# Moving whole expert sets into the last two thirds of the following row's slot

## The chip, the cores and the metric

The kernel runs on one core of a Trainium2 chip. The core has four engines that compute: TensorE (PE in the profile, with its weight loads as PEld), VectorE (DVE), ScalarE (ACT) and GpSimd (POOL). SyncE (SP) issues nearly all of this kernel's transfers. Each engine works through its own queue in order and waits on semaphores that the others raise. The metric is the time of one launch in microseconds (us) on the device. Three runs of the kernel before gave 1374.11, 1378.02 and 1379.18 us, a median of 1378.02 us.

## The reference

The input is 4 rows of 512 tokens with 128 channels, all fp32. Two layers are applied. Cut to what matters here:

```python
xn = layernorm(x)                                   # layer 0
x  = x + band_attention(xn) + gated_experts(xn)     # 16 heads, window of 64; 16 experts, top 4
xn = layernorm(x)                                   # layer 1
x  = x + full_attention(xn) + relu_experts(xn)      # 16 heads, 512 keys; 8 experts, top 2

def relu_experts(xf):
    score = relu(xf @ rw1 + rb1) @ rw2 + rb2
    gate  = softmax(top 2 of score)                 # 0 for the other six experts
    out   = sum over e of gate[:, e] * (relu(xf @ W1[e] + b1[e]) @ W2[e] + b2[e])
```

In the band attention of layer 0 the logit of a query and each of its 64 predecessors is not a dot product: it goes through two GELU networks on the difference of two 16-vectors per head. So each row needs 64 large subtractions on VectorE and as many GELUs on ScalarE. The relu experts of layer 1 are 4 hidden blocks and 4 second products for each of 8 experts and each row, all computed for every token, with the gate deciding what counts.

## The kernel before

Everything is laid out by row of the batch. A row's relu experts and its full attention belong to layer 1, but both need only this row's finished layer 0 result, so the kernel starts the experts of one row while the next row's layer 0 is under way.

The work is written as Python generators, each of which yields after a small step. `weave` (L92, `woven` at L80) takes pairs of a generator and a number of steps and interleaves them in proportion, so that all end together. A generator that has made its number of steps is left where it is and can be continued in a later weave. The tile framework gives each instruction a priority by its place in this program order; a planner then puts the ready instructions of each engine into its queue by priority, using its own estimates of durations. Instructions can so move ahead of their place when an engine would be free. The small products of the band logits (L574) are lifted in priority by `tc.high_priority` (L570). Once the queues are written they are run strictly in order.

The generators:

- `band_logits(b)` (L543): 64 steps, each one subtraction on VectorE (L560), its GELU on ScalarE (L562 or L566) and four small products on TensorE (L574). Then a maximum, an exponential (L616, L620) and the write of the weights to DRAM, `by_t` (L621).
- `band_values(b)` (L304): needs `by_t`. For each of four token tiles: eight loads `f` from `by_t` (L312), transposes (L321), copies `g` (L322), a write to `by_s` (L327), loads `wb` in skewed order (L338), products with the values (L348, L352). 14 steps; it ends in `add_rows`.
- `gated_experts(b)` (L647): layer 0's 16 experts, one step each (L674, L681, L659 to L663), with loads of `wT` (L630) and of the routes (L672).
- `prepare(b)` (L492): norms, projections and routes of layer 0, 6 steps.
- `relu_experts(b)` (L392): layernorm and transposes, the router (L381 with `rw1`, L406), the routes (L416), then the experts: each step makes one hidden block (`hidden`, L378: a 128x512 product at L381 and a relu at L389) for expert e and one second product (L442) for expert e-1. Expert e loads `w1` (L428), `w2` (L430) and its route `r` (L432). After each expert VectorE weighs the result (L446) and GpSimd adds it up (L447). In layer 0 the generator makes 3 steps before the experts and 36 for them. In layer 1, where the list `pace` is in use, each of the 36 is two steps, and the hidden products are tied to the attention's steps.
- `full_attention()` (L769): layer 1's attention for all rows, with an order of products written out by hand. A step makes score products of one pair for the maxima (`m`) and of another for the exponentials (`x`) (L920), VectorE takes maxima (L936), ScalarE exponentials (L942), and every other step multiplies by the values (L838).

The PSUM banks that `bank()` (L107) hands out are two, shared by the relu experts, the band values, the preparation and the transposes. `full_attention` has its own six.

A row's slot in layer 0 is two weaves, `first` and `second` (L719 to L734). From row 1 on, `first` holds 30 steps of the row's own band logits, 7 gated experts and all band values of the row before. `second` holds the other 37 steps of logits, 10 of gated experts, the preparation of the next row and 20 steps of the relu experts of the row before. The remaining 21 steps of those experts lie in `first` of one slot later, or, for row 2, in layer 1: there they are woven with the band values of row 3, and the experts of row 3 follow (L950 to L953). "First part" and "second part" below mean these two weaves.

Of the kernel before, what the change touches and what calls it, by code (L numbers as in the profile page):

```python
# [29 lines left out]
B, T, C = 4, 512, 128  # L30
# [49 lines left out]
def woven(*tracks):  # L80


    live = [[g, n, 0] for g, n in tracks]
    while live:
        t = min(live, key=lambda v: (v[2] + 1) / v[1])
        t[2] += 1
        if next(t[0], "end") == "end" or t[2] == t[1]:
            live.remove(t)
        yield


def weave(*tracks):  # L92
    for _ in woven(*tracks):
        pass
# [3 lines left out]
def two_layers(ctx: ExitStack, tc: tile.TileContext, w: dict, consts: bass.AP, out: bass.AP):  # L98
# [8 lines left out]
    def bank():  # L107
        return ps_f.tile([P, 512], FP, tag="f", name="bank")
# [16 lines left out]
    def c_(name):  # L125
        return cst[:, offs[name][0]:offs[name][1]]
# [80 lines left out]
    def layernorm(b, dst, pin=False):  # L207

        mv = small.tile([P, TPB, 2], FP, tag="mv", name="mv")
        for i in range(TPB):  # L210
            st = small.tile([P, 6], FP, tag="st", name="st")
            ins = nc.vector.bn_stats(st, x1[:, b * TPB + i, :])
            if pin and not i:
                tc.keep_in_program_order(ins)
            nc.vector.bn_aggr(mv[:, i, :], st)
        rs = inv_sqrt(mv[:, :, 1], 1.0)
        for i in range(TPB):
            nc.vector.tensor_scalar(
                dst[:, i, :], x1[:, b * TPB + i, :], mv[:, i, 0:1], rs[:, i:i + 1],
                ALU.subtract, ALU.mult,  # L220
            )
# [9 lines left out]
    def transposed(src):  # L231

        pt = bank()
        for i in range(TPB):
            nc.tensor.transpose(pt[:, i * P:(i + 1) * P], src[:, i, :], ident)
        return pt

    def routes(pool, tag, g, n, k, less, dst):


        shape = [P, TPB, n, n]
        both = pool.tile([P, 2, TPB, n * n], FP, tag=tag, name="both")
        gt, eq = both[:, 0], both[:, 1]
        other = g[:, :, None, :].to_broadcast(shape)
        own = g[:, :, :, None].to_broadcast(shape)
        gt4 = gt.rearrange("p t (a b) -> p t a b", a=n)
        eq4 = eq.rearrange("p t (a b) -> p t a b", a=n)
        nc.vector.tensor_tensor(gt4, other, own, ALU.is_gt)
        nc.vector.tensor_tensor(eq4, other, own, ALU.is_equal)
        nc.vector.tensor_tensor(eq, eq, less[:, None, :].to_broadcast([P, TPB, n * n]), ALU.mult)  # L250
        nc.vector.tensor_tensor(gt, gt, eq, ALU.add)
        rank = small.tile([P, TPB, n], FP, tag=f"rank{n}", name="rank")
        nc.vector.tensor_reduce(rank, gt4, AX.X, ALU.add)
        nc.vector.tensor_scalar(rank, rank, float(k), None, ALU.is_lt)
        mx = small.tile([P, TPB], FP, tag="rmx", name="rmx")
        nc.vector.tensor_reduce(mx, g, AX.X, ALU.max)
        nc.vector.tensor_tensor(dst, g, mx[:, :, None].to_broadcast([P, TPB, n]), ALU.subtract)
        nc.scalar.activation(dst, dst, AF.Exp)
        nc.vector.tensor_tensor(dst, dst, rank, ALU.mult)
        nc.vector.tensor_reduce(mx, dst, AX.X, ALU.add)  # L260
        nc.vector.reciprocal(mx, mx)
        nc.vector.tensor_tensor(dst, dst, mx[:, :, None].to_broadcast([P, TPB, n]), ALU.mult)
# [18 lines left out]
    def add_rows(b, py):  # L281
        nc.vector.tensor_tensor(rows_of(b), rows_of(b), py, ALU.add)
# [95 lines left out]
    def hidden(wt, bias, b, c):  # L378

        ph = bank()  # L380
        mm = nc.tensor.matmul(ph, wt[:, c * P:(c + 1) * P], xT[:, b * T:(b + 1) * T], start=True, stop=True)  # L381
        if pace:
            tc.add_manual_dep(
                mm.ins, pace[-1].ins.name,
                mybir.DependencyInfo(mybir.DependencyClass.NoSync, mybir.DependencyReason.DATA),
                reason="experts spread over the steps",
            )
        h = chain.tile([P, T], FP, tag="h", name="h", bufs=5)
        nc.scalar.activation(h, ph, AF.Relu, bias=bias[:, c:c + 1])  # L389
        return h  # L390

    def relu_experts(b):  # L392


        xn = chain.tile([P, TPB, C], FP, tag="o", name="xn", bufs=1)
        layernorm(b, xn)
        pt = transposed(xn)
        nc.scalar.copy(xT[:, b * T:(b + 1) * T], pt)
        yield
        rw1 = chain.tile([C, F1], FP, tag="ew1", name="rw1")  # L400
        nc.sync.dma_start(out=rw1, in_=w["L1_ffn_rw1"])
        hs = [hidden(rw1, cols[:, 32:36], b, c) for c in range(4)]
        pg = bank()
        for i in range(TPB):
            for c in range(4):
                nc.tensor.matmul(  # L406
                    pg[:, i * E1:(i + 1) * E1], hs[c][:, i * P:(i + 1) * P], rw2[:, c, :],
                    start=(c == 0), stop=(c == 3),
                )
        scores = small.tile([P, TPB, E1], FP, tag="scores1", name="scores1")  # L410
        nc.vector.tensor_tensor(
            scores, pg[:, :TPB * E1].rearrange("p (t e) -> p t e", e=E1),
            rb2[:, None, :].to_broadcast([P, TPB, E1]), ALU.add,
        )
        route = small.tile([P, TPB, E1], FP, tag="route1", name="route1")
        routes(small, "pairs", scores, E1, K1, c_("lt8"), route)  # L416
        yield
        rT = route_rows(small, route, E1, route_d[1][b], 1.0)
        py = bank()
        nc.tensor.matmul(py, b2_1, rT, start=True, stop=True)  # L420
        total = chain.tile([C, T], FP, tag="total", name="total", bufs=1)
        nc.scalar.copy(total, py)
        yield
        old = None
        for e in range(E1 + 1):
            if e < E1:
                w1 = chain.tile([C, F1], FP, tag="ew1", name="ew1")
                nc.sync.dma_start(out=w1, in_=w["L1_ffn_W1"][e])  # L428
                w2 = chain.tile([P, 4, C], FP, tag="ew2", name="ew2")
                nc.sync.dma_start(out=w2, in_=w["L1_ffn_W2"][e].rearrange("(c p) d -> p c d", p=P))  # L430
                r = chain.tile([P, T], FP, tag="r", name="r")
                nc.sync.dma_start(out=r, in_=route_d[1][b][e].partition_broadcast(P))  # L432
            new = []
            if old:
                py = bank()
            for c in range(4):
                if e < E1:
                    new.append(hidden(w1, cols[:, e * 4:e * 4 + 4], b, c))
                if pace:
                    yield  # L440
                if old:
                    nc.tensor.matmul(py, old[1][:, c, :], old[0][c], start=(c == 0), stop=(c == 3))  # L442
                yield
            if old:
                part = chain.tile([C, T], FP, tag="part", name="part", bufs=1)
                nc.vector.tensor_tensor(part, py, old[2], ALU.mult)  # L446
                nc.gpsimd.tensor_tensor(total, total, part, ALU.add)  # L447
            old = (new, w2, r)
        pt = transposed(total.rearrange("p (t c) -> p t c", t=TPB))
        add_rows(b, pt)  # L450
        yield

    def after(*parts):
        for p in parts:
            yield from p


    with ExitStack() as l0:
# [31 lines left out]
        ready = {}  # L490
# [223 lines left out]
        nc.vector.tensor_scalar_add(b_lin, gbt[:, 2, :], -LIMIT)  # L714

        experts = {}
        for b in range(B):  # L719
            logits_b, gated_b = band_logits(b), gated_experts(b)  # L720
            if not b:
                weave((logits_b, 6), (preparation, 4))
            first = [(logits_b, 30 if b else 24), (gated_b, 7)]
            second = [(logits_b, 37), (gated_b, 10)]
            if b:
                first.append((band_values(b - 1, ready[b - 1][1]), 14))
                experts[b - 1] = relu_experts(b - 1)
                second.append((experts[b - 1], 20))
            if b > 1:
                first.append((experts[b - 2], 21))  # L730
            if b + 1 < B:
                second.append((prepare(b + 1), 6))
            weave(*first)
            weave(*second)  # L734
# [34 lines left out]
    def full_attention():  # L769
# [179 lines left out]
    x_out = out.rearrange("b (t p) c -> p b t c", p=P)  # L949
    weave(  # L950
        (full_attention(), 106),
        (after(woven((band_values(B - 1, ready[B - 1][1]), 14), (experts[B - 2], 41)), relu_experts(B - 1)), 13 + 40 + 76 + 4),
    )  # L953
    nc.sync.dma_start(out=x_out[:, B - 1], in_=x1[:, (B - 1) * TPB:B * TPB, :])

# [33 lines left out]
```

## Time and profile before

The profiled execution took 1381.3 us, of which 1379.5 us are the span of the core; the median of the runs is 1378.02 us.

| stretch (us from the span's start) | what runs there | PE busy | DVE busy | ACT busy |
|---|---|---|---|---|
| 0 to 237 | start, slot of row 0 | 164.29 | 209.56 | 198.80 |
| 237 to 472 | slot of row 1 | 191.75 | 200.77 | 204.83 |
| 472 to 706 | slot of row 2 | 207.15 | 210.11 | 210.78 |
| 706 to 940 | slot of row 3, change to layer 1 | 205.32 | 194.08 | 200.56 |
| 940 to 1120 | attention, band values of row 3, rest of row 2's experts | 160.28 | 86.01 | 76.47 |
| 1120 to 1360 | attention, experts of row 3 | 233.56 | 109.41 | 120.06 |

The stretches of layer 0 are cut where the exponentials of a row (begun by L616 at 228, 465, 699 and 925 us) have just been written. A busy time is the union of an engine's instructions and says nothing of what it could have done faster. A 128x512 fp32 product shows as two records, so a count of x2 at L381, L442, L674 or L681 is one product; the transposes and the small products with `wb` show as one.

### The profile page before, as it was taken

How to read it: one execution, taken by the hardware profiler on the slowest of the kernel's cores; microseconds unless marked ns; L12 is line 12 of the kernel's file. 1: busy time of each engine (PE TensorE's matmuls, PEld its weight loads, DVE VectorE, ACT ScalarE, POOL GpSimd, SP SyncE). 2: the span in 40 equal slices, each digit the busy share in tenths (PEclk: the TensorE clock that was granted, in tenths of full speed). 3: DMA queues.
4: the chain of work that ended last, by engine and by line, in shares of the span. 5: the costliest groups of instructions: out<-in, count | busy, mean ns of one | idle time of the engine just before them, and what ended most of it. 6: DMA issues, size and time to landing. Idle time of an engine off the chain costs nothing.

```text
span 1379.5 us, 17426 instructions
## 1 busy us (share of the span) xinstructions
PE 1174.3 (85%) x6763; PEld 450.2 (33%) x6763; DVE 1012.4 (73%) x1085; ACT 1018.5 (74%) x1160; POOL 96.9 (7%) x68
## 2 busy tenths in 40 slices
PE   5676976678889789889989988887999899999997
PEld 2122323123433323353333334232333332333322
DVE  4999998999866999987799998843444434444451
ACT  4899997999968899988889988862454435545554
POOL 2000000000000002200002320012000000000000
PEclk9799998899879999999999999999999989999999
DMA  7121213446212445622244751235133200011100
GB/s 268 44 74 52 76 52 103 100 118 153 62 41 75 150 102 145 170 64 64 73 153 110 180 131 48 67 96 166 49 88 77 69 9 24 24 38 39 31 16 8
DMA packets 168524, 117.61 MB, mean 85 GB/s; under 512 B 66621, under 2 KB 149274, under 8 KB 166906
## 3 DMA queue, kind: packets, MB, share of 16 engines
q1 hardware_dynamic: 166970, 109.77, 29.3%
q0 software_dynamic: 1184, 6.29, 1.2%
q8 instruction: 54, 0.88, 0.3%
q10 hardware_dynamic: 288, 0.43, 0.1%
q14 instruction: 28, 0.23, 0.1%
HBM read 89.00 MB, written 27.46 MB: 84 GB/s over the span
## 4 chain that ended last, share of the span: by engine, by line
PE 59%; ACT 17%; DVE 13%; DMA 6%; issue 5%; SPq 0%; DVEq 0%; ACTq 0%
PE score L920 11%; PE lbank L574 10%; PE bank L381 8%; PE bank L442 7%; ACT z L566 6%; DVE z L560 5%; PE accbank L838 4%; ACT z L562 3%; PE gbank L674 3%; PE accbank L663 3%; DMA wb<-by_s 3%; PE gbank L681 2%; DMA wT<-wT_all 2%; DVE nmax L936 2%; PE abank L810 1%
## 5 line engine op out<-in xcount | busy, mean ns | idle before, releaser
L560 DVE TENSOR_TENSOR z<-proj 128x2044 f32<-128x2044 f32 (+31 forms) x256 | 554.1, 2189 | 29.0 <-PE lbank L574 12.6
L574 PE MATMUL lbank<-z,place 128*32 128x504 f32 (+18 forms) x2048 | 288.9, 639 | 110.1 <-ACT z L566 68.8
L936 DVE TENSOR_REDUCE nmax<-score 128x2 f32<-128x1024 f32 x128 | 156.3, 1225 | 182.3 <-PE score L920 180.1
L566 ACT ACTIVATE z<-z,posb 128x1024 f32<-128x1024 f32 (+31 forms) x256 | 267.3, 1097 | 10.2 <-DVE z L560 8.2
L942 ACT ACTIVATE ex<-score 128x1024 f32<-128x1024 f32 x128 | 130.3, 1023 | 159.7 <-PE score L920 159.7
L562 ACT ACTIVATE z<-z,brep 128x2048 f32<-128x2048 f32 (+31 forms) x128 | 241.4, 1906 | 5.3 <-DVE z L560 4.9
L920 PE MATMUL score<-k,q 32*128 32x512 f32 x512 | 152.2, 655 | 13.9 <-DVE nmax L936 11.7
L447 POOL TENSOR_TENSOR total<-total,part 128x512 f32<-128x512 f32 x32 | 82.6, 2580 | 1038.3 <-DVE part L446 1038.3
L920 PE MATMUL score<-qa,k 32*128 32x512 f32 x512 | 139.7, 648 | 2.1 <-ACT ex L942 2.1
L381 PE MATMUL bank<-xT,ew 128*128 128x512 f32 x256 | 136.2, 626 | 1.6 <-ACT h L389 0.8
L442 PE MATMUL bank<-h,ew 128*128 128x512 f32 x256 | 133.1, 619 | 4.7 <-issue 4.7
L389 ACT ACTIVATE h<-bank,cols 128x512 f32<-128x512 f32 x144 | 97.1, 684 | 45.3 <-PE bank L381 44.6
L574 PEld LDWEIGHTS lbank<-z,place 128*32 128x32 f32 x2048 | 43.0, 112 | 264.2 <-ACT z L566 143.9
L663 PEld LDWEIGHTS accbank<-wT,lin 128*128 128x128 f32 x512 | 72.2, 204 | 60.4 <-issue 34.6
L663 PE MATMUL accbank<-wT,lin 128*128 128x128 f32 x512 | 82.1, 297 | 10.1 <-DVE lin L661 10.1
L674 PE MATMUL gbank<-tT,wT 128*128 128x512 f32 x128 | 72.2, 647 | 17.4 <-DMA wT<-wT_all 16.5
L838 PE MATMUL accbank<-ex,vaug 128*32 128x512 f32 x512 | 70.8, 619 | 0.2 <-ACT ex L942 0.2
L681 PE MATMUL gbank<-tT,wT 128*128 128x512 f32 x128 | 70.6, 635 | 0.0
L920 PEld LDWEIGHTS score<-k,q 32*128 32x128 f32 x512 | 41.2, 187 | 89.0 <-ACT ex L942 44.1
L442 PEld LDWEIGHTS bank<-h,ew 128*128 128x128 f32 x256 | 44.2, 193 | 74.4 <-issue 71.0
L381 PEld LDWEIGHTS bank<-xT,ew 128*128 128x128 f32 x256 | 41.9, 192 | 72.8 <-issue 43.6
L659 DVE SCALAR_TENSOR_TENSOR lin<-lin,r 128x512 f32<-128x512 f32 x64 | 44.5, 695 | 28.6 <-ACT lin L683 28.3
(188 smaller groups left out, 1193.7 us busy)
## 6 DMA issues: line engine op xcount, KB each, us to landing
r<-route SPq DMA_DIRECT2D x96, 256.0 KB, 3.5
ew<-in_L_ffn_W SPq DMA_DIRECT2D x64, 256.0 KB, 3.4
wb<-by_s SPq DMA_DIRECT2D x32, 512.0 KB, 4.1
wT<-wT_all SPq DMA_DIRECT2D x48, 192.0 KB, 3.0
by_t<-e SPq DMA_DIRECT2D x8, 1024.0 KB
f<-by_t SPq DMA_DIRECT2D x128, 64.0 KB, 3.1
by_s<-g SPq DMA_DIRECT2D x16, 512.0 KB, 4.2
wb<-by_s SPq DMA_DIRECT2D x24, 256.0 KB, 3.6
```

Of the source, the lines that this page charges most:

```text
L381: mm = nc.tensor.matmul(ph, wt[:, c * P:(c + 1) * P], xT[:, b * T:(b + 1) * T], start=True, stop=True)
L442: nc.tensor.matmul(py, old[1][:, c, :], old[0][c], start=(c == 0), stop=(c == 3))
L560: nc.vector.tensor_tensor(z[:, :, :, 0:n], seen, own, ALU.subtract)
L562: nc.scalar.activation(z[:, :, :, 0:n], z[:, :, :, 0:n], AF.Gelu, bias=b_dmg)
L566: last = nc.scalar.activation(z[:, dq, :, 0:n], z[:, dq, :, 0:n], AF.Gelu, bias=posb[:, j:j + 1])
L574: mm = nc.tensor.matmul(ps[q:q + 32, t0:T], place[:, kind, 3 - dd:35 - dd], z[:, dq, hg, 0:n], start=(dd == 0), stop=(dd == 3),)
L663: nc.tensor.matmul(ya[:, i * P:(i + 1) * P], lin[:, i * P:(i + 1) * P], wT[:, 2, :], start=False, stop=(e == E0 - 1 and i == TPB - 1),)
L674: nc.tensor.matmul(pg, wT[:, 0, :], tT, start=True, stop=True)
L838: mm = nc.tensor.matmul(av[n][r:r + 32, :], vaug[b % 2][:, i, g * 4 + h, :], ex[n, i][:, h, :], start=(i == 0), stop=(i == TPB - 1),)
L920: mm = nc.tensor.matmul(ps[:, h - two, :], own[r, i * P:(i + 1) * P], seen[r, :], start=True, stop=True)
L936: freed.append(nc.vector.tensor_reduce(nmax[n % 2][:, i, two:two + 2, 8:9], ps, AX.X, ALU.max, negate=True))
L942: freed.append(nc.scalar.activation(ex[n, i][:, two:two + 2, :], ps, AF.Exp, scale=inv))
```

## The change

Each row's relu experts are no longer cut in two. All of their 41 steps go into `second` of the following row's slot. `first` holds the band values of the row before, the gated experts and, from row 1 on, 22 steps of the logits where it held 30; `second` holds 45 where it held 37. In layer 1 only row 3's band values and experts are left beside the attention, first the one, then the other, and the number that the weave is told falls from 133 to 93.

```diff
-        experts = {}
         for b in range(B):
             ...
-            first = [(logits_b, 30 if b else 24), (gated_b, 7)]
-            second = [(logits_b, 37), (gated_b, 10)]
+            first = [(logits_b, 22 if b else 24), (gated_b, 7)]
+            second = [(logits_b, 45), (gated_b, 10)]
             if b:
                 first.append((band_values(b - 1, ready[b - 1][1]), 14))
-                experts[b - 1] = relu_experts(b - 1)
-                second.append((experts[b - 1], 20))
-            if b > 1:
-                first.append((experts[b - 2], 21))
+                second.append((relu_experts(b - 1), 41))
             ...
     weave(
         (full_attention(), 106),
-        (after(woven((band_values(B - 1, ready[B - 1][1]), 14), (experts[B - 2], 41)), relu_experts(B - 1)), 13 + 40 + 76 + 4),
+        (after(band_values(B - 1, ready[B - 1][1]), relu_experts(B - 1)), 13 + 76 + 4),
     )
```

For row 0 nothing is moved: its logits are 24 and up to 45 steps, of which 37 are left.

## The prediction

> **What bounds the kernel now.** I read the slices first, then the busy time by slot and by part of a slot, then who waits for whom in each part, and last the attention's steps in order of time.
>
> ```profile
> PE   5676976678889789889989988887999899999997
> DVE  4999998999866999987799998843444434444451
> ACT  4899997999968899988889988862454435545554
> ```
>
> A slice is 34.5 us. Up to slice 27 (layer 0) VectorE and ScalarE are at 80 to 90% or more with dips, from there on (layer 1) TensorE alone is full. So there are two regimes, and a TensorE microsecond has a different price in each. In the next rows the columns are: stretch, length, busy PE, PEld, DVE, ACT, POOL, then clock and DMA. First three whole slots, then first part and second part of slot 1, of slot 2, and the second part of slot 3.
>
> ```profile
> 237.00:472.00 235.00, 191.75 (x1145) 76.82 (x1144) 200.77 (x215) 204.83 (x221) 4.30 (x4) 0.90 0.37 98
> 472.00:706.00 234.00, 207.15 (x1223) 87.73 (x1222) 210.11 (x223) 210.78 (x236) 28.93 (x8) 0.96 0.41 112
> 706.00:940.00 234.00, 205.32 (x1186) 83.26 (x1185) 194.08 (x186) 200.56 (x219) 37.25 (x14) 0.96 0.43 119
> ...
> 250.00:351.00 101.00, 74.61 (x659) 28.40 (x659) 98.81 (x80) 95.51 (x97) 0.00 (x0) 0.93 0.51 122
> 351.00:472.00 121.00, 107.45 (x446) 45.68 (x445) 90.11 (x129) 96.35 (x115) 4.30 (x4) 0.89 0.23 65
> 484.00:600.00 116.00, 102.43 (x755) 41.07 (x754) 111.73 (x89) 109.67 (x120) 23.09 (x4) 0.97 0.52 130
> 600.00:706.00 106.00, 95.72 (x430) 43.76 (x429) 86.37 (x129) 89.14 (x108) 4.19 (x3) 0.95 0.25 76
> ...
> 834.00:940.00 106.00, 92.57 (x395) 39.63 (x394) 70.64 (x92) 78.95 (x92) 8.20 (x9) 0.95 0.30 91
> ```
>
> A first part is VectorE's (98.81 of 101, 111.73 of 116): the subtractions set the pace. A second part is TensorE's (95.72 of 106), with VectorE a fifth idle. Slot 1's first part carries no experts, and its TensorE is idle a quarter of the time; slot 2's carries half a set, and only 12% is idle. All slots have one length.
>
> In the attention a step lasts from one score product to the next:
>
> ```profile
> 1226.66 0.70 PE L920 MATMUL score<-k,q 32*128 32x512 f32 x2
> ...
> 1227.73 1.12 PE L442 MATMUL bank<-h,ew 128*128 128x512 f32 x2
> ...
> 1228.70 1.02 PE L381 MATMUL bank<-xT,ew 128*128 128x512 f32 x2
> ...
> 1229.65 0.70 PE L920 MATMUL score<-k,q 32*128 32x512 f32 x2
> ...
> 1241.39 0.70 PE L920 MATMUL score<-k,q 32*128 32x512 f32 x2
> ...
> 1242.46 1.06 PE L838 MATMUL accbank<-ex,vaug 128*32 128x512 f32 x8
> ...
> 1243.94 0.70 PE L920 MATMUL score<-k,q 32*128 32x512 f32 x2 [0.41 <-DVE nmax L936]
> ```
>
> Two expert products take 1227.73 to 1229.65, so 0.96 us each. The step with both lasts 2.99 us. The step with the value products alone lasts 2.55 and ends in a wait for the maximum: 2.55 is a floor, and a first product in a step without value products costs nothing, a second 0.44, one beside value products 0.57 (3.12 less 2.55).
>
> **The change, part by part.** What moves is the second half of a set. The first 20 steps are 3 of the router and 17 of experts; left are 15 hidden blocks and 19 second products, 34 x 0.96 = 32.6 us of TensorE; 15 relus at 0.68 us (L389) = 10.2 of ScalarE; 5 weighings at 0.69 (L446) = 3.5 of VectorE; 5 adds on GpSimd; 9 loads on SP's queue (`w1`, `w2`, `r` of experts 5 to 7). Slot 1 gets one such half more. Slots 2 and 3 give one from the first part and get one in the second. Layer 1 loses one.
>
> *Layer 1.* Of row 2's 34 products 23 stand between 947 and 1115 us, the other 11 before, while the attention still waits for its memsets and first operands; those 11 bring nothing. I went through the 23 by step: the usual saving is 0.44 or 0.57 us, about 1 where the step also holds a query or key product, 1.9 in one step of 4.42, and 0 for four. The sum is 12.9 us. Row 3's 68 products are then spread over more steps: the weave gives 93/106 = 0.88 of their steps per attention step where it gave 1.25. Eight steps around 1290 us with 7 expert products lasted 25.45 us, and 21.3 without by the floor and the rows above, 0.5 a product; spread thinner more of them are a step's free first. I put 0.4, over 64 expert products 6 us. Against it, row 3's band values now run within 14/0.88 = 16 yields of 4.1 us, some 66 us, where the trace has 940 to 1115. The chain of waits there holds waits for `by_s` (4.14 and 4.08) and `wb` (6.84, 6.19 and 4.04), 25 us in all, that fewer expert products now fill: 0 to 8 more, I take 3. Layer 1: -12.9 - 6 + 3 = -16, between -8 and -25.
>
> *The slots.* I count TensorE's time as occupied (to the next start, at most 0.62 us a record) and idle. Slot 1 has 187.6 occupied, slot 2 211.2, slot 3 207. Expert products took 34.2 us of slot 1 and 63.6 of slot 2, so a moved half is 29.4 us by this count. Idle in the parts: 23.5 us in slot 1's first, 10.7 and 11.1 in those of slots 2 and 3, 18.5, 9.6 and 13.9 in the second ones; the hand-over between slots holds some 3.
> First part after: VectorE's work is 22 subtractions at 2.29 us with their share of small ones, 7 gated experts at 3 x 0.69 and 3 us for the band values: 50 + 15 + 3 = 68 us. The band values' chain of transfers (8 issues of `f` at 0.6 us, `g`, 4.2 for `by_s`, 4.1 to 7 for `wb`, the products) is some 16 us for each of four tiles, so 65 us at least; in slot 1 it took 101. I take 75. TensorE without experts idles there as in slot 1, 23.5/101 = 23%: 17 us.
> Second part after: all 68 expert products behind a router that takes 36 us from the layernorm (600) to the first hidden block (636). Idle stays near 9.6, slightly more for its greater length: 11 in slots 1 and 2, 14 in slot 3.
> Slot 1: 187.6 + 29.4 + 3 + 17 + 11 = 248, now 235: +13. Slot 2: 211.2 + 31 = 242, now 234: +8. Slot 3: 207 + 34 = 241, now 234: +7. Sum +28; between 0 (slot 1 takes the half into its idle quarter) and +64 (the band values take 101 us as now, so the idle is 24 for each slot, +21, and the queue below, +15).
>
> *Queues.* In the second part SP's queue already stands at L630 for 23.5 us (slot 2) and 26.4 (slot 3) and at L428 for 18.9 and 15.3:
>
> ```profile
> SPq L630 <- PE accbank L663: 23.5, 7, 8.2
> SPq L428 <- PE bank L381: 18.9, 4, 8.2
> ...
> SPq L430 <- PE bank L442: 9.1, 3, 5.7
> ```
>
> A load of `w1` that waits for its buffer holds up the `wT` and route loads behind it, for which L674 waits 8.4 us as weight load in slot 1 and 3.2 in slot 2. Nine more expert loads per second part cost 0 to 5 a slot; I take 0, since the gated experts' ten loads are also spread over more time, and leave 5 to the range. The five adds leave a part where GpSimd needed up to 9.5 us for one (1.27 in layer 1); worth under 1 us. The 10.2 us of relus go to slot 1, where ScalarE has 30 us idle: nothing, if it is idle when they come; at full price they are 10, inside the upper end.
>
> [...] All three slots last 234 or 235 us although slots 2 and 3 hold some 29 us more of TensorE than slot 1: by this row an added half costs a slot nothing, and the sum would be -16. [...] experts leave the part that VectorE bounds for the one that TensorE bounds. [...] slot 2's equal length came with experts in both parts, and that is what goes.
>
> **Sum.** The profiled execution was 1381.3 us: + 28 - 16 = 1393. Its median of runs is 3.3 lower, so 1390.
>
> **Rivals.**
> 1. *The slots absorb the experts* (ends faster). The planner lets logits run ahead: at 351 us, where 30 were due, some 40 of slot 1's steps were done. If logits run ahead through the second part and leftover experts fill the next first part, no slot grows: 1378 - 16 = 1362. For it: equal slots; the raised priority of L574. Against it: in slot 2's second part no subtraction (L560) began between 660 and 678 us, while experts and preparation ran on TensorE. It decides if the three slots together grow by less than 9 us.
> 2. *Both sides cancel.* Slots grow by 9 to 23: 1371 to 1385.
> 3. *Band values do not shorten and SP's queue holds the gated experts up.* +28 and +21 for the idle, and half of the queue's price, 7, make slots +56: 1378 + 56 - 16 = 1418. For it: 101 us in slot 1 even without experts beside them. Against it: VectorE was full in that time, so the pace was that of the logits.
>
> **How the numbers follow.** About 0.5%, 7 us, is what a measurement can tell from no change. Likeliest case (slots +23 to +45, own range 1385 to 1407): 0.54. Rival 1: 0.22. Rival 2: 0.14. Rival 3: 0.10. Slower 0.54 + 0.10 = 0.64, same 0.14, faster 0.22. Low end 1358 is rival 1 with a better layer 1 (-20), high end 1420 rival 3 with its queue; what lies beyond is under 2 in 10.
>
> **What would show it.** Right: slots of about 248, 242 and 241 us; first parts near 75 us with VectorE full and TensorE a quarter idle; second parts near 155 with TensorE over 90%; the stretch from the fourth exponential to the end some 16 us shorter. Wrong: slots still of 234 (rival 1), or a layer 1 that doesn't shrink because its steps sit on the 2.55 floor or the band values' waits come to the front. If slot 1's first part is still 100 us, the chain of transfers and not VectorE set it.

## The result: 7.8% slower, and the profile after

The changed kernel takes 1485.03 us (median; 1480.93 to 1486.77) where the kernel before takes 1378.02: a ratio of 1.0778, 95% interval 1.0754 to 1.0802. The sign of the forecast was right; the size, +12 us, was not: +107 us lies far outside 1358 to 1420. The profiled execution has a span of 1480.3 us, 100.8 more than before, and by that the time is divided here.

The slices of the page first, in the same order as before: TensorE, VectorE, ScalarE.

```profile
PE   5686776878899767889977778995879999999996
DVE  5999979999656799966479997623422445554551
ACT  4899978998876799978588997932232454454544
```

A slice is now 37 us. VectorE no longer stays near full in layer 0: the seventh to tenth slices stand at 9 and the next three at 6, 5 and 6, and again in the slots that follow, where three slices at 9 are followed by 6, 6 and 4. TensorE does the opposite: 8, 9 and 9 where VectorE has 6, 6 and 4. The two regimes, which lay side by side in each slot before, have moved further apart.

I cut each slot at two events that both kernels have: the subtraction before the exponentials (L616), and the last copy of the band values (L369), after which the second part can start its layernorm. A first part cut so begins 19 to 22 us earlier than the windows of the prediction (484 and 250 us against L616 at 465 and 228) and ends 2 or 3 us earlier. The columns are as before: stretch, length, busy PE, PEld, DVE, ACT, POOL, clock, DMA. First the kernel before, first and second part of slot 2:

```profile
465.00:597.00 132.00, 114.01 (x786) 44.46 (x785) 129.02 (x96) 125.17 (x129) 24.75 (x5) 0.97 0.54 143
597.00:699.00 102.00, 93.13 (x438) 43.26 (x437) 81.08 (x127) 85.87 (x107) 4.19 (x3) 0.95 0.24 73
```

Then the changed kernel, first and second part of slots 1, 2 and 3:

```profile
220.00:349.00 129.00, 96.23 (x718) 40.39 (x716) 123.08 (x103) 113.24 (x119) 0.00 (x0) 0.85 0.51 131
349.00:497.00 148.00, 138.51 (x562) 59.48 (x562) 97.09 (x141) 110.81 (x136) 14.26 (x9) 0.94 0.27 75
497.00:618.00 121.00, 87.41 (x695) 32.95 (x693) 117.36 (x88) 109.84 (x105) 0.00 (x0) 0.83 0.47 124
618.00:759.00 141.00, 130.95 (x516) 55.05 (x516) 84.98 (x131) 104.12 (x130) 12.22 (x8) 0.95 0.27 78
759.00:881.00 122.00, 87.62 (x709) 33.19 (x708) 120.58 (x93) 113.28 (x109) 0.00 (x0) 0.86 0.49 126
881.00:1011.00 130.00, 121.24 (x472) 49.32 (x470) 72.87 (x97) 88.30 (x109) 10.15 (x8) 0.96 0.26 76
```

In slot 2 TensorE is busy for 87 of 121 us in the first part and for 131 of 141 in the second; VectorE for 117 and 85. The same cuts give this account, in us:

| stretch | before | after | difference |
|---|---|---|---|
| start to first L616 | 228 | 220 | -8 |
| first parts of slots 1, 2, 3 | 120, 132, 132 | 129, 121, 122 | +9, -11, -10 |
| second parts of slots 1, 2, 3 | 117, 103, 94 | 148, 141, 130 | +31, +38, +36 |
| last L616 to the end | 455 | 470 | +15 |

The half set that comes to a second part is 34 products by the program, 32.6 us of TensorE. Each second part grows by about that, and so does TensorE's busy time in it: by 34, 38 and 38 us (from 104.84, 93.13 and 83.21). The first parts that lost a half shrink by a third of it. Slot 1's, which lost none, is 9 us longer and the start 8 us shorter: row 0's band values end at 349 us in both kernels, and only L616 has moved. Layer 1 lost a half set as well, and it is longer.

### The profile page after: what moved, and what is told of

Its sections match the earlier page's. It is cut to its first block, busy times and chain, and to the rows that moved or that the text cites. A ratio compares the mean times of both kernels' runs of the same rounds, so it can differ in the third digit from the quotient of the medians.

```text
span 1480.3 us, 17438 instructions
## 1 busy us (share of the span) xinstructions
PE 1230.2 (83%) x6763; PEld 468.6 (32%) x6763; DVE 1004.6 (68%) x1085; ACT 1024.3 (69%) x1161; POOL 61.2 (4%) x68
## 4 chain that ended last, share of the span: by engine, by line
PE 61%; ACT 17%; DVE 12%; DMA 5%; issue 4%; POOLq 0%; POOL 0%; SPq 0%; DVEq 0%; ACTq 0%
PE lbank L574 11%; PE score L915 10%; PE bank L381 9%; PE bank L442 8%; ACT z L566 6%; ACT z L562 4%; DVE z L560 4%; PE accbank L663 4%; PE gbank L674 3%; PE accbank L833 3%; DVE nmax L931 3%; PE gbank L681 2%; DMA wT<-wT_all 2%; PE bank L235 1%; PE bank L406 1%
## 5 line engine op out<-in xcount | busy, mean ns | idle before, releaser
L560 DVE TENSOR_TENSOR z<-proj 128x2044 f32<-128x2044 f32 (+31 forms) x256 | 551.9, 2175 | 30.5 <-PE lbank L574 19.5
L574 PE MATMUL lbank<-z,place 128*32 128x504 f32 (+18 forms) x2048 | 306.2, 671 | 125.6 <-ACT z L562 62.1
L915 PE MATMUL score<-k,q 32*128 32x512 f32 x512 | 158.2, 675 | 15.1 <-DVE nmax L931 13.9
L915 PE MATMUL score<-qa,k 32*128 32x512 f32 x512 | 148.3, 661 | 4.7 <-ACT ex L937 4.7
L663 PE MATMUL accbank<-wT,lin 128*128 128x128 f32 x512 | 90.3, 318 | 20.1 <-DVE lin L661 20.0
L663 PEld LDWEIGHTS accbank<-wT,lin 128*128 128x128 f32 x512 | 77.1, 219 | 82.7 <-issue 39.7
L674 PE MATMUL gbank<-tT,wT 128*128 128x512 f32 x128 | 77.0, 686 | 22.9 <-DMA wT<-wT_all 21.4
L447 POOL TENSOR_TENSOR total<-total,part 128x512 f32<-128x512 f32 x32 | 46.7, 1461 | 1168.5 <-DVE part L446 1168.5
L681 PE MATMUL gbank<-tT,wT 128*128 128x512 f32 x128 | 74.2, 664 | 0.0
L446 DVE TENSOR_TENSOR part<-bank,r 128x512 f32<-128x512 f32 x32 | 22.0, 689 | 76.5 <-PE bank L442 76.5
L677 ACT ACTIVATE glu<-gbank,gbt 128x512 f32<-128x512 f32 x64 | 43.9, 686 | 34.4 <-PE gbank L674 33.9
```

The source lines that it names most:

```text
L560: nc.vector.tensor_tensor(z[:, :, :, 0:n], seen, own, ALU.subtract)
L574: mm = nc.tensor.matmul(ps[q:q + 32, t0:T], place[:, kind, 3 - dd:35 - dd], z[:, dq, hg, 0:n], start=(dd == 0), stop=(dd == 3),)
L663: nc.tensor.matmul(ya[:, i * P:(i + 1) * P], lin[:, i * P:(i + 1) * P], wT[:, 2, :], start=False, stop=(e == E0 - 1 and i == TPB - 1),)
L674: nc.tensor.matmul(pg, wT[:, 0, :], tT, start=True, stop=True)
L915: mm = nc.tensor.matmul(ps[:, h - two, :], own[r, i * P:(i + 1) * P], seen[r, :], start=True, stop=True)
```

## Experiments

Below, first and second parts are those of slots 1 to 3 by the cuts above.

### Which part of the edit: numbers or whole sets

```diff
-            first = [(logits_b, 30 if b else 24), (gated_b, 7)]
-            second = [(logits_b, 37), (gated_b, 10)]
+            first = [(logits_b, 22 if b else 24), (gated_b, 7)]
+            second = [(logits_b, 45), (gated_b, 10)]
```

> The kernel before with the changed numbers alone: 22 and 45 steps of logits for 30 and 37, the sets of experts still cut in two. Theory (the four tiles of the band values are a chain of about 25 us each that sets the length of the first part, and logits run ahead of their number anyway, so the loss comes from where the experts' products stand): 1378, within 8. Rival (the 22 steps take work away from the first part): a good part of the 107 us, 1400 or more.

1401.65 us, ratio 1.0181 (1.0149 to 1.0213). The rival's 1400 is reached, but 23 us are under a quarter of the 107: the numbers count, and are not the main part. Slot 0 ends 11 us earlier (L616 at 217 us), slots 1 and 2 take 247 each for 237 and 234, and layer 1 takes 463 for 455.

The other way, the changed kernel with 30 and 37:

```diff
-            first = [(logits_b, 22 if b else 24), (gated_b, 7)]
-            second = [(logits_b, 45), (gated_b, 10)]
+            first = [(logits_b, 30 if b else 24), (gated_b, 7)]
+            second = [(logits_b, 37), (gated_b, 10)]
```

> The changed kernel with the old numbers, 30 and 37, and whole sets in the second part. Theory: 1485, within 8. Rival (the numbers matter): 1460 or less.

1475.18 us, 10 less than 1485, which lies between theory and rival. So whole sets cost 97 with the old numbers (1475.18 less 1378.32, the kernel before measured beside it), and the numbers 10 on top. The first parts of slots 2 and 3 take 122 and 120 us, as long as with 22 steps; slot 1's takes 120 and the start 229, as before. Here nothing but experts has moved, so this run gives their price: the first parts that lost a half are 9 and 12 us shorter than in the kernel before, and the second parts 24, 40 and 34 us longer.

The dose: half of the move, old numbers.

```diff
-                second.append((experts[b - 1], 20))
+                second.append((experts[b - 1], 31))
             if b > 1:
-                first.append((experts[b - 2], 21))
+                first.append((experts[b - 2], 10))
...
-        (after(woven((band_values(B - 1, ready[B - 1][1]), 14), (experts[B - 2], 41)), relu_experts(B - 1)), 13 + 40 + 76 + 4),
+        (after(woven((band_values(B - 1, ready[B - 1][1]), 14), (experts[B - 2], 21)), relu_experts(B - 1)), 13 + 20 + 76 + 4),
```

> The kernel before, its own 30 and 37, with 31 steps of a set in the second part and 10 in the next first part or in layer 1, so about half of what the change moves. Theory (each product that goes to the second part is paid there, and the first part keeps its length): about half of the 97 that whole sets cost with the old numbers, 1378 + 40 to 55 = 1418 to 1433. Rival (a threshold: the second part takes some more products free): under 1400.

1438.51 us, 1.0431 (1.0400 to 1.0463): 62 us, over half of the 97 and over the range expected. No threshold: the first 11 steps cost more than the next ten. First parts 120, 125, 123, second parts 130, 132, 119.

### Is TensorE's time in a first part free?

The changed kernel, with a half set of the row two before computed again beside the band values of slots 2 and 3 and thrown away:

```diff
+            if b > 1:
+                first.append((half_again(b - 2), 21))
```

`half_again` makes the expert steps 4 to 8 of `relu_experts` without the add on GpSimd (16 hidden blocks, 16 second products, their relus, loads and weighings).

> The changed kernel with such a half set of the row two before computed once more in the first parts of slots 2 and 3, beside the band values, 64 products in all and thrown away. Theory (the first part's length is the band values' chain, its TensorE time is free): within 8 of 1485. Rival (TensorE's time counts wherever it stands): 64 x 0.96 more, 1546.

1504.58 us. 64 products are 61 us of TensorE; they cost 20. Not free, but a third of the price. The first parts of slots 2 and 3 go from 121 and 122 to 135 and 134. The window of slot 2's first part shows where the rest went:

```profile
498.00:633.00 135.00, 114.77 (x785) 42.05 (x783) 128.48 (x98) 127.70 (x129) 0.00 (x0) 0.92 0.48 130
```

TensorE is busy for 115 of 135 us where it had been 87 of 121: 27 us more work in 14 us more time. The same third appears in the account above with the other sign: a half set taken out of a first part shortened it by 10 or 11 us, and one put into a second lengthened it by 31 to 38 (9 to 12 and 24 to 40 where nothing but experts moved).

### What holds a first part at 120 us

My sum had 75 us, which is 91 to 95 from L616 to the last copy. Three links were tried. First, nearly all logits out of the first weave:

```diff
-            first = [(logits_b, 22 if b else 24), (gated_b, 7)]
-            second = [(logits_b, 45), (gated_b, 10)]
+            first = [(logits_b, 1 if b else 24), (gated_b, 7)]
+            second = [(logits_b, 66), (gated_b, 10)]
```

> The changed kernel with 1 step of logits in the first weave of rows 1 to 3 and 66 in the second, so nearly nothing but the band values and 7 gated experts stands before the second part in the order. If the number of logits beside them sets the pace: first parts (from the exponentials to the end of the band values) of 90 us or less. If the chain or the planner's running ahead does: 115 to 130 as now. The time for either: 1450 to 1500, since what leaves the first part comes back in the second.

1481.16 us, first parts of 138, 118 and 122. The number has hardly any hold on the first part: slot 1's is 9 us longer, the others are as they were. The subtractions of the logits (L560) in slot 2's first part tell why. These are the kernel before with 30 steps in that weave, the changed one with 22, and this one with 1; the figures are length, VectorE's time in these subtractions and their count.

```profile
465.00:597.00 132.00, 104.35 (x47) 0.97 0.54 143
497.00:618.00 121.00, 96.79 (x45) 0.83 0.47 124
502.00:620.00 118.00, 95.42 (x44) 0.88 0.51 130
```

So some 45 steps run there, whatever the number.

Second, a PSUM bank of their own for the sums of the band values and the transposes of these, in layer 0, taken from the gated experts (three banks to two):

```diff
-            acc = bank()
+            acc = vbank()
...
-            pt = transposed(avs)
+            pt = transposed(avs, vbank)
...
-        ps_g = l0.enter_context(tc.tile_pool(name="ps_g", bufs=3, space=PSUM))
+        ps_g = l0.enter_context(tc.tile_pool(name="ps_g", bufs=2, space=PSUM))
+        own_bank.append(l0.enter_context(tc.tile_pool(name="ps_v", bufs=1, space=PSUM)))
```

> The changed kernel with one PSUM bank more for layer 0's band values: their sums and the transposes of these take it in turn, and no longer share the two banks that the transposes of the next tile need. The gated experts have two banks for three. Theory (the rotation of two banks chains the tiles): a tile takes some 16 us instead of 25.5, the first part shrinks by up to 35 us in each of three slots, VectorE then being the bound, and the time falls to 1400 to 1440. Rival (each tile's own transfers or the planner's order set 25 us): 1485 or more.

1474.77 us, 10 less, first parts 128, 118 and 119. The banks are a small link; the theory that they chain the tiles falls. The same edit in the kernel before:

> The same bank in the kernel before. Theory: the first part is VectorE's there (111.73 of 116 us busy) and holds experts as filler, so a shorter chain gives little: 1365 to 1385. Rival (each tile's own transfers): 1378 or some us more, since the gated experts lose a bank.

1369.65 us, 0.9939 (0.9926 to 0.9952): a small gain.

Third, the way through DRAM cut: `wb` read from `by_c`, a tensor filled with ones at the start, so the band values' weights are left out of the result.

```diff
-                    at = by_s.offset + s * P * H * BW + half * 8 * BW + (0 if own else P)
+                    at = by_c.offset + s * P * H * BW + half * 8 * BW + (0 if own else P)
```

> The changed kernel, where the loads wb of the band values read a DRAM tensor filled once at the start instead of by_s, so they need not wait for the write of by_s (its values are then not the reference's). Theory (the chain sets the first part): 4 to 8 us less a tile, 16 tiles, so 1360 to 1420. Rival (VectorE's logits set the first part, the chain has slack): within 8 of 1485.

1459.39 us. First parts of 117, 108 and 108, so 12 to 14 us shorter, second parts of 152, 148 and 135, so 4 to 7 longer; layer 1, whose band values are cut too, is 11 us shorter and the start 12 us longer. The chain does hold the first part, by less than I expected, and nearly half of what it gives up comes back in the second. The edit takes away what `wb` must wait for, but not the order of SP's queue, in which these loads still stand behind the write of `by_s`. That write waits for the copies `g` of ScalarE; in slot 2's first part, of the changed kernel and of this one:

```profile
SPq L327 <- ACT g L322: 23.1, 3, 11.9
...
SPq L328 <- ACT g L323: 42.1, 4, 13.5
```

Both cuts at once:

> The changed kernel with both links cut: wb read from a constant tensor (its values are then not the reference's) and the own bank. If these two links are the chain: first parts of 85 to 95 us for 121 and 108 with the first cut alone, and a time of 1430 to 1450, half of the gain being given back in the second part as in the run with one cut. If not: first parts of 105 and 1450 to 1460.

1470.95 us, with runs from 1451.51 to 1472.08. First parts 92, 103 and 109; second parts 160, 151 and 134. The three slots together are 42 us shorter than in the changed kernel, but slot 0 ends at 265 us instead of 220. The edit did more than it was meant to. With `wb` constant and a bank of their own, row 0's band values need no logits any more, and the planner put their products at the very start, from 46 to 71 us. VectorE waits for their sums, and the first subtraction of the logits (L572 in this run) stands behind them. It begins at 72.6 us, where the changed kernel has it at 21.6:

```profile
50.54 0.26 DVE L367 RECIPROCAL rd<-vbank 128x16 f32<-128x16 f32 x1 [25.75 <-PE vbank L235]
...
72.61 8.87 DVE L572 TENSOR_TENSOR z<-proj 128x2048 f32<-128x2048 f32 x4
```

So its 92 us are no measure of a chain, and for the time it decides nothing.

What remains of the 120 us stays open in its shares. In the changed kernel's slot 2 the first write of `by_s` is issued 32 us after L616 and the others 20, 26 and 22 us later. Writing and rereading it is one link. The order that the planner gave to transposes, copies and loads is another, and so is VectorE's own queue: its 45 subtractions alone are 97 us. Whether VectorE fills the time of a chain or the last sums stand behind the subtractions, no run here separates.

### Layer 1: fewer products, more time

The kernel before, with the second half of row 2's set left out of layer 1 and computed nowhere (19 steps of it in slot 3 instead of 20, so that no sum is left open):

```diff
-                second.append((experts[b - 1], 20))
+                second.append((experts[b - 1], 20 if b < B - 1 else 19))
...
-        (after(woven((band_values(B - 1, ready[B - 1][1]), 14), (experts[B - 2], 41)), relu_experts(B - 1)), 13 + 40 + 76 + 4),
+        (after(band_values(B - 1, ready[B - 1][1]), relu_experts(B - 1)), 13 + 76 + 4),
```

> The kernel before with the second half of row 2's experts (some 35 products, 0.96 us each) left out of layer 1 and computed nowhere; the weave there is told 93 steps. Prediction's step (layer 1 gives back 16 us when it loses the half): 1362. Theory (beside row 3's band values these products stood in waits, and without them the clock falls): within 6 of 1378.

1391.02 us, 1.0093 (1.0070 to 1.0117). About 35 products less, and 14 us more. From 939 to 1032 us, beside the band values, the granted clock was 0.70, where the kernel before has 0.96. And the changed kernel with a half set of row 2 computed once more there and thrown away, woven as in the kernel before:

```diff
-        (after(band_values(B - 1, ready[B - 1][1]), relu_experts(B - 1)), 13 + 76 + 4),
+        (after(woven((band_values(B - 1, ready[B - 1][1]), 14), (half_again(B - 2), 41)), relu_experts(B - 1)), 13 + 40 + 76 + 4),
```

> The changed kernel with a half set of row 2 (16 hidden blocks and 16 second products, loads and relus too; the sum is thrown away) computed once more beside row 3's band values in layer 1, as the kernel before does with the real one. Theory (free filler there): 1485 or less. Rival (0.5 us a product, as along the later steps): 1500.

1471.30 us: 32 products more, 14 us less. Two readings were left, that the products are useful filler, or that what counts is the pace of the band values. This one gives the pace without a product:

```diff
+    def pause(n):
+        for _ in range(n):
+            yield
...
-        (after(band_values(B - 1, ready[B - 1][1]), relu_experts(B - 1)), 13 + 76 + 4),
+        (after(woven((band_values(B - 1, ready[B - 1][1]), 14), (pause(40), 41)), relu_experts(B - 1)), 13 + 40 + 76 + 4),
```

> The changed kernel, with row 3's band values in layer 1 spread over as many steps of the attention as before, by empty steps in the place of the half set: no product more, only the pace. Theory A (crowded, the four tiles' chains hold the attention up: 5.4 us a step for 17 steps): 14 to 35 us less, 1450 to 1471. Theory B (the products themselves are needed, since without them the granted clock falls to 0.72 there): 1485, within 6.

1454.63 us, 30 less than the changed kernel: the pace. The products are not free there either: the repeated half costs 17 us more than the pauses alone (1471.30 less 1454.63), 0.5 us a product. From the last L616 to the end this run takes 441 us, where the changed kernel takes 470, the kernel before 455, and the one with the repeated half 460. The windows from the attention's first score product to the last copy of the band values, of the kernel before, of the changed one, and of the one with the pauses (the last column but two is the granted clock):

```profile
947.00:1107.00 160.00, 145.85 (x970) 52.40 (x966) 77.61 (x83) 68.18 (x87) 3.83 (x3) 0.96 0.31 76
```

```profile
1031.00:1122.00 91.00, 77.96 (x481) 31.04 (x480) 32.19 (x36) 22.49 (x33) 0.00 (x0) 0.73 0.44 103
```

```profile
1032.00:1153.00 121.00, 97.90 (x748) 37.41 (x745) 58.07 (x63) 45.77 (x59) 0.00 (x0) 0.91 0.32 77
```

Of the attention's 1024 score records (8 to a step) some 384, 136 and 288 lie in them: 3.3 us a step, 5.4 and 3.4. The timeline of the changed kernel at the fourth tile shows a wait and a slower TensorE behind it:

```profile
1102.49 0.70 PE L915 MATMUL score<-k,q 32*128 32x512 f32 x2 [0.40 <-DVE nmax L931]
...
1103.56 0.65 PE L787 MATMUL abank<-cst,avs 128*128 128x128 f32 x4
...
1104.74 2.15 SPq L338 DMA_DIRECT2D wb<-by_s  x3
...
1108.72 0.65 PE L348 MATMUL bank<-wb,va 128*32 128x128 f32 x8 [4.51 <-DMA wb<-by_s]
...
1110.16 2.07 PE L915 MATMUL score<-k,q 32*128 32x512 f32 x2
...
1123.48 1.12 PE L915 MATMUL score<-k,q 32*128 32x512 f32 x2
...
1133.29 3.78 PE L381 MATMUL bank<-xT,rw 128*128 128x512 f32 x4
```

The products with `wb` stand in TensorE's queue ahead of the next scores and wait for a load that has just been issued, so the scores wait with them, 4.51 us. After that the score product at 1110.16 takes 2.07 us, at a granted clock of 0.50; one at 1123.48, also with no other beside it, takes 1.12, and from 1124 to 1130 the clock is 1.00. Two products of the router take 3.78 at 1133.29, with a clock of 0.50 from 1131 to 1136, where an expert product of the same shape takes 0.96 at 1.00 (the kernel before, 1227.73 to 1229.65). The granted clock (last column but two) of the changed kernel is at half over whole stretches. Behind these two rows stand TensorE's waits for `wb` in the crowded stretch and in the one with the pauses (total, times, longest):

```profile
1045.00:1065.00 20.00, 18.90 (x71) 7.21 (x71) 6.88 (x8) 2.34 (x4) 0.00 (x0) 0.50 0.41 98
1107.00:1123.00 16.00, 14.28 (x88) 5.61 (x88) 1.77 (x3) 2.19 (x3) 0.00 (x0) 0.50 0.29 70
...
PE bank L348 <- DMA wb<-by_s: 6.7, 2, 4.5
...
PE bank L348 <- DMA wb<-by_s: 6.2, 3, 3.1
```

The waits are nearly the same with the pauses, so they are not the price. The whole of layer 1 shows what is, in the changed kernel and with the pauses:

```profile
1011.00:1480.00 469.00, 411.80 (x2275) 140.84 (x2274) 199.26 (x233) 199.84 (x240) 15.94 (x15) 0.90 0.15 41
1012.00:1453.00 441.00, 381.10 (x2276) 130.12 (x2274) 198.56 (x233) 200.11 (x240) 15.97 (x15) 0.94 0.16 44
```

TensorE has the same work (2275 and 2276 records) and is idle for 57 and 60 us; it is busy for 412 and 381. So the 28 us are products that take longer. Taken us by us, the granted clock of the changed kernel here is 1.00 in 365 of the 469 us, 0.50 in 91 and between in 13. By these two levels, taken for both runs, means of 0.90 and 0.94 are some 94 and 53 us at half: 41 us more, worth about 20 (an estimate from these rows: at half, 41 us hold what takes some 20 at full, and the score products above took 2.07 and 1.12 us). The other 10 are not accounted for. Why the clock stays down in the crowded stretch is open: at 1107 it is already at half, less than 3 us into the wait, and from 1045 to 1065 it is at half though TensorE counts as busy for 18.90 of 20 us.

### A better version

If second parts are TensorE's and first parts take products at a third of the price, the split should move the other way. With the band values' own bank:

```diff
-                second.append((experts[b - 1], 20))
+                second.append((experts[b - 1], 16))
             if b > 1:
-                first.append((experts[b - 2], 21))
+                first.append((experts[b - 2], 25))
...
-        (after(woven((band_values(B - 1, ready[B - 1][1]), 14), (experts[B - 2], 41)), relu_experts(B - 1)), 13 + 40 + 76 + 4),
+        (after(woven((band_values(B - 1, ready[B - 1][1]), 14), (experts[B - 2], 49)), relu_experts(B - 1)), 13 + 48 + 76 + 4),
```

> The other way, with the band values' own bank: 16 steps of a set in the second part, 25 in the next first part or in layer 1. Theory (second parts are TensorE's, first parts have it idle for a tenth): some us under the 1370 of the kernel with the bank alone, 1355 to 1370. Rival (the first part, 112 of 116 us VectorE's, has no room left): 1372 to 1385.

1358.86 us, 0.9862 (0.9843 to 0.9881): the fastest kernel here, 18 us under the kernel before, of which the bank alone had given 9. First and second part of slot 2, in which TensorE is now busy for 89% of both (86 and 91% before):

```profile
447.00:582.00 135.00, 120.46 (x798) 44.90 (x796) 130.78 (x98) 125.95 (x130) 22.67 (x6) 0.96 0.53 144
582.00:684.00 102.00, 90.75 (x432) 40.85 (x429) 79.93 (x129) 86.40 (x108) 2.55 (x2) 0.95 0.23 69
```

One step further, 12 and 29 (and 57 and 56 in layer 1):

> The band values' own bank with 12 steps of a set in the second part and 29 in the next first part or in layer 1. If second parts are still TensorE's and first parts still take products below their price: 1345 to 1358. Rival (with 25 steps the first part was full already, and layer 1 pays for its longer half): 1360 to 1372.

1363.80 us, 0.9920 (0.9897 to 0.9942), as the rival had it. Second parts go on shrinking (99, 99, 81 for 100, 102, 90), but layer 1 grows from 459 to 465 us and the medians say that the best is near 16.

## Why the prediction was wrong

Two steps failed: the length of the first part without experts, and the price of crowded band values in layer 1. The slots grew by 94 us for a forecast of 28, layer 1 by 15 for -16, and the start, which was not in the sum, shrank by 8.

**The first part (failed).** "I take 75." It was put above VectorE's work (68) and a chain of "some 16 us for each of four tiles" (65), and is 91 to 95 us from L616 to the last copy. Measured: 129, 121 and 122. Both terms were wrong. VectorE's 68 us counted 22 steps of logits, but the planner fills an idle VectorE with whatever logits are ready: 45 subtractions, 97 us, run in slot 2's first part, and a weave with 1 step for 22 leaves 44. The number in a weave is a priority, not a share of time; I had seen 40 for 30 in the trace and used it for a rival only. The chain is 20 to 26 us a tile after a start of 32. The upper bound that I had named, 101 us "as now", was near the value of all slots (121 from L616 in slot 1 before). The sentence that went with it, that a first part of 100 us would mean the chain sets it and not VectorE, was borne out in part: one link, cut, gave 12 to 14 us a slot, and what sets the rest is open.

**The second part (too long, on the way to a total too short).** Slots of 248, 242 and 241 less 95, 91 and 91 leave 153, 151 and 150; measured 148, 141 and 130. That fits the same failure: with more logits done in the first part than I counted, fewer were left. It gave back 5 to 20 of the 30 to 34 us that the first parts were short. The slots came to 277, 262 and 252. That TensorE bounds the second part was right: it is busy for 131 of 141 us in slot 2.

**The idle TensorE of slot 1 in every slot (right, undersized).** By the windows above (length less busy PE) the first parts of slots 2 and 3 have 34 us of it each where I put 17, because I took the part for 75 us long. Slot 1's had 33 of 120 before by the same cut. The second parts have 10 and 9 for 11 and 14.

**Layer 1, the moved products (right in kind, somewhat large).** The step by step sum gave -12.9 and -6, so -19; with the pauses the stretch goes from 455 to 441 us: -14. A repeated half costs 0.5 us a product there, near the 0.44 and 0.57 of the sum. (The 0.5 a product of the eight steps around 1290 us was itself 4.15 over 7, so 0.6.)

**Layer 1, the crowding (failed).** "0 to 8 more, I take 3." It is 29 (470 less 441). I priced the waits alone, and took it that the attention would run on beside them. The waits for `wb` on TensorE are indeed alike, 6.7 us crowded and 6.2 with the pauses. What I had at nothing is how fast TensorE works: for the same products it is busy 31 us longer, some 20 of them, by the estimate above, for a clock that is at half for 41 us more.

**The queue and the relus (right).** L674 waits for `wT` in slot 1's second part 6.3 us as weight load and 7.4 as product, where it was 8.4 and 4.8: much the same in all. ScalarE stays under full in the second parts (110 of 148).

**Equal slots.** Equal slot lengths had said that a half set costs nothing. Not to rely on them was right; the price that I put instead was my own estimate and much too small. The size came with the runs: with nothing else moved, a half set cost 9 to 12 us in a first part and 24 to 40 in a second.

**The rivals.** Rival 1 (slots absorb) and rival 2 fell. Rival 3 had the mechanism, band values that don't shorten, but not SP's queue, and at +56 for the slots it was under the +94 measured; it also kept the -16 for layer 1.

## What to carry to other kernels

Before work is moved within a pipelined schedule, ask of each stretch what ends it: a stretch that is held by something else shrinks little when an engine's work leaves it (10 us for 33 here), and a stretch that this engine fills grows by about all that comes to it (31 to 38 for 33). Numbers in an order that a planner may overtake do not set lengths; look in the trace at how far the work had in fact run ahead, and use that in the sum. And where the products of a chain share a queue with a busy loop, try spreading the chain out: here it left the waits as they were and took 31 us off TensorE's busy time. Lastly, an edit that cuts a dependency also frees the planner: see where the work has gone before the time is read.

## What was not expected of the hardware

With four tiles of band values crowded into 91 us TensorE had a mean granted clock of 0.73, spread over 121 us one of 0.91, though it was idle for a smaller share of the crowded stretch (13 of 91 us, 23 of 121). So leaving work out made a run longer (1391.02 for 1377.37) and adding 32 thrown-away products made one shorter (1471.30 for 1485.03): they set the pace of the band values beside them.
